# Normalised rows and contexts transposed by VectorE and small transfers instead of TensorE, in a four-layer transformer kernel

## The chip, the cores and the metric

The kernel runs on one core of one Trainium2 chip. The metric is the device time of one execution in microseconds. A core has a matrix engine (TensorE, PE in the profile), a vector engine (VectorE, DVE), an activation engine (ScalarE, ACT), a general engine (GpSimd, POOL), and SyncE (SP), whose queue only issues transfers (DMAs) here. Each engine works through its own instructions in order; semaphores tie the engines to each other.

## The reference

`x` holds 4 batches of 256 tokens with 256 features, `ctx` 4 contexts of 512 tokens with 128 features. Four layers each add a cross-attention and a feed-forward block, both on the normalised rows:

```python
x = x + L0_xattn(layernorm(x), ctx)   # 16 heads of 16, normalised q and k, last 16 context tokens apart
x = x + L0_ffn(layernorm(x))          # 64 "arrows" of rank 16, the 4 longest of each token, and a dense base
x = x + L1_xattn(layernorm(x), ctx)   # 16 heads of 128 on 8 key heads
x = x + L1_ffn(layernorm(x))          # 8 experts, the best 2 of each token, and a shared one
x = x + L2_xattn(layernorm(x), ctx);  x = x + L2_ffn(layernorm(x))   # the better of two experts
x = x + L3_xattn(layernorm(x), ctx);  x = x + L3_ffn(layernorm(x))   # the best 64 tokens of each batch
```

`layernorm` subtracts a row's mean and divides by its standard deviation. All of it is in float32. What matters here: each of these blocks needs the normalised rows with the features on the partitions (a matrix product sums over the partitions), while they are normalised with the tokens on the partitions. Each of the 8 normalised sets of rows must be transposed, batch by batch, and so must each context, once.

## The kernel before

All inputs, the rows `x_sb[b]` (128 partitions x 2 chunks of tokens x 256) and the contexts `c_sb` stay in on-chip memory (SBUF); only weights, and rows for the gathers of the experts, pass through DMA. The order of work on TensorE, ScalarE, VectorE and GpSimd is the order in which `bounded_path` (L837) issues it, by hand. SyncE's order is set by the framework's scheduler, by when a transfer's sources are expected. Transfers of SyncE use eight semaphores in turn, so at most eight are on their way.

**The transposes.** `Norm` (L914) computes a batch's statistics: four small operations of VectorE (L924, L925), one more for the epsilon (L926), and a power on GpSimd (L927). `Norm.tokens` (L929) writes the normalised rows `xn` with two VectorE operations, into a ring of two buffers (pool `lnp`, tag "xn"). `layernorm_T` (L938) transposes them: four matrix products with the identity of 128x128 each (L944) into a PSUM bank, and one ScalarE copy (L947) to `xnT` (128 features x 2 x 256 tokens; a ring of two, tag "xnT"). `context_T` (L906) does the same to a context: four transposes (L910), one copy to `cT`.

**Layer 0, attention.** The loop over batches b and steps i = 0 to 7 issues, in each step, `scores` of half a group of heads (L1371; matrix products L1378, exponentials on ScalarE), the values of the step before (L1388), every second step `quotient` (L1405; VectorE transposes L1411, L1415, multiplication L1419), and then `between(b, i)` (L1589), which prepares batch n = b + 1. For n = 2 and 3, `between` has: at the last two steps of the batch before `Norm` and `tokens`, at i = 0 the transposes of context (`context_T`, then `last_context`, L1176, two GpSimd copies) and of the rows, at i = 1 `project_q` (L1184, products L1189), at i = 2 `project_k` (L1200), at i = 6 `transposed` (L1337; its VectorE part L1353). For n = 1, rows and context are transposed ahead, in part at i = 0. `output0` (L1426) adds a batch's result to `x_sb` (L1438).

**Layer 0, feed-forward.** `Arrows` (L1448; `vectors` with products L1462, `routes`, `turned`, `output` L1512) works on 8 chunks of 128 tokens. Its rows are transposed for batch 0 at (b, i) = (3, 3), batch 1 at (3, 5), batches 2 and 3 in the loop that follows, at n = 1 and 3. Folding of layer 1's weights (L981, `fold`) fills in.

**Layers 1 to 3, attention.** `attention` (L1795) runs over 32 units (b, hp), 4 batches by 8 pairs of heads. A unit takes some 8.4 us and has, on TensorE, `queries` (`seven`, L1893: a 2x2 block product with seven products in place of eight), four scores of 128x512 (L1923) and four products with the context (L1931). For the next batch: `Norm` at hp = 1, `tokens` at hp = 3, `layernorm_T` at hp = 5, `x_sums` (L1855, sums of blocks of `xnT` for `seven`) at hp = 6; `queries` of the next batch follow at hp = 7. VectorE has per unit a transpose of 128x512 (L1952) and sums (L1950, L1956).

**Layer 1, feed-forward.** Its preparation for batches 0 to 2 stands beside layer 1's attention (`beside1`, L2248): `Norm` at hp = 3, `tokens` at hp = 4, `turned1` (L2189) at hp = 5, which stores the rows to `xd` in device memory (L2190) and transposes them (L2195, copy L2196), and at hp = 6 `chosen` (L2198), which computes the gate's products and picks two experts. Batch 3 follows after the attention.

Of the kernel before, what the change touches and what calls it, by code (L numbers as in the profile page):

```python
# [9 lines left out]
F32 = mybir.dt.float32  # L10
# [826 lines left out]
def bounded_path(ctx: ExitStack, tc: tile.TileContext, t, out: bass.AP, over):  # L837
# [8 lines left out]
    first = ctx.enter_context(ExitStack())  # L846
    f0w = first.enter_context(tc.tile_pool(name="f0w", bufs=1, side="right"))
    w0 = first.enter_context(tc.tile_pool(name="w0", bufs=2, side="right"))
    ring = first.enter_context(ExitStack())
    ringo = ctx.enter_context(ExitStack())  # L850
    banks = {
# [99 lines left out]
        xn = Norm(b, name).tokens(keep)  # L951
        return xn, layernorm_T(xn, name)

    def normalised(name):

        after = layernorm(0, f"{name}_0")
        for b in range(B):
            _, xnT = after
            if b + 1 < B:
                after = layernorm(b + 1, f"{name}_{b + 1}")  # L960
            yield b, xnT

    raws = {}

# [68 lines left out]
    with tc.manual_schedule(engines={E.PE, E.Activation, E.DVE, E.Pool}):  # L1033
# [545 lines left out]
        def ahead(b, i):  # L1579

            n = b + 1
            if n < B:
# [3 lines left out]
                elif i == 7 and n > 1:  # L1586
                    transposed(n, 4)

        def between(b, i):  # L1589

            n = b + 1
            if n == 1:
                if i == 0:
                    for k0 in range(0, NK, 2):
                        project_k(n, k0)()
                    scale[n] = Scale(n)
                    scale[n].square(False, NC, NQK)
                    xnTs[n] = layernorm_T(xns[n], f"a0_{n}")
                elif i == 1:
                    project_q(n)()  # L1600
                    scale[n].square(False, 0, NC)
                    project_v(n)
                elif i == 2:
                    scale[n].sum()
                    scale[n].power()
                elif i == 5:
                    transposed(n, 0)
                    transposed(n, 2)
                elif i == 6:
                    transposed(n, 4)  # L1610
            elif n < B:
                if i == 0:
                    context_T(n)
                    last_context(n)
                    xnTs[n] = layernorm_T(xns[n], f"a0_{n}")
                elif i == 1:
                    project_q(n)()
                elif i == 2:
                    for k0 in range(0, NK, 2):
                        project_k(n, k0)()  # L1620
                    scale[n] = Scale(n)
                    scale[n].square(False)
                elif i == 3:
                    project_v(n)
                    scale[n].sum()
                elif i == 4:
                    scale[n].power()
                elif i == 6:
                    transposed(n, 0)
                    transposed(n, 2)  # L1630
            if n + 1 < B:
                if i == (5 if n == 1 else 6):
                    norms[n + 1] = Norm(n + 1, f"a0_{n + 1}")
                elif i == (6 if n == 1 else 7):
                    xns[n + 1] = norms[n + 1].tokens()

            i0 = 4 if b == B - 1 else 6
            if b > 0 and i in (i0, i0 + 1):
                output0(b - 1, (i - i0,))
            if b == 1:  # L1640
                if i == 0:
                    bias_rows()
                elif i == 1:
                    bias_columns()
                elif i == 2:
                    output_bias()
            if b == B - 1:
                if i == 0:

                    mf = w0.tile([B * NK, P], F32, tag="hs", name="mf", bufs=1)  # L1650
                    nc.vector.tensor_copy(mf, m8)
                    xns["mf"] = mf
                elif i == 1:
                    pmk = bank("mm", [P, B * NK], "pmk")
                    nc.tensor.transpose(pmk, xns["mf"], ident[: B * NK, : B * NK])
                    nc.vector.tensor_scalar(
                        mbias.rearrange("p b k -> p (b k)"), pmk, 1.0, -NEG, ALU.subtract, ALU.mult
                    )
                elif i == 2:
                    score_bound()  # L1660
                elif i == 3:

                    nc.vector.tensor_reduce(
                        quad[:, :32], ident.rearrange("p (a q) -> p q a", q=32), AX.X, ALU.add
                    )
                    for j in range(1, 4):
                        nc.vector.tensor_copy(quad[:, 32 * j : 32 * (j + 1)], quad[:, :32])
            if b == B - 1:
                if i in (0, 2, 6):
                    norms["f", i // 2] = Norm(min(i // 2, 2), f"f0_{min(i // 2, 2)}")  # L1670
                if i in (1, 3, 7):
                    xns["f", i // 2] = norms["f", i // 2].tokens()
                if i in (3, 5):
                    k = (i - 3) // 2
                    xnTs["f", k] = layernorm_T(xns["f", k], f"f0_{k}")
                if i == 4:
                    arrows[0] = Arrows(0)
                    arrows[0].vectors()
                if i == 5:
                    arrows[0].routes()  # L1680
# [43 lines left out]
        for n in range(B * NC):  # L1724
            if n + 2 < B * NC:
                arrows[n + 2].routes()
            if n:
                arrows[n].turned()
            if n % NC == 0:
                if n + 3 < B * NC:  # L1730
                    arrows[n + 3] = Arrows(n + 3)
                    arrows[n + 3].vectors()
                for _ in range((0, 0, 1, 1, 2, 2, 1, 1)[n]):
                    next(fold)
                if n == 6:
                    xn1 = norm.tokens()
                if n:
                    arrows[n].output()
            else:
                k = n // NC + 2  # L1740
                if k < B:
                    xnTs["f", k] = layernorm_T(xns["f", k + (k == 2)], f"f0_{k}")
                if n == 7:
                    first_xnT = layernorm_T(xn1, "a1_0")
                    next(fold)
                arrows[n].output()
                for _ in range((0, 0, 1, 1, 2, 2, 1, 0)[n]):
                    next(fold)
                if n + 3 < B * NC:
                    arrows[n + 3] = Arrows(n + 3)  # L1750
                    arrows[n + 3].vectors()
            if n == 5:
                norm = Norm(0, "a1_0")
            if n == 0:
                norm = Norm(3, "f0_3")
            if n == 1:
                xns["f", 3] = norm.tokens()
            if 2 <= n < 2 + B:

                b = n - 2  # L1760
                c2 = w0.tile([P, NK, DC], F32, tag="z0", name=f"c2_{b}")
                for k in range(NK):
                    nc.scalar.activation(
                        c2[:, k], c_sb[:, b, k], AF.Square, accum_out=csq[:, b * NK + k : b * NK + k + 1]
                    )
# [29 lines left out]
    def attention(L, m_sb, n_sb, first_xnT=None, after=None, at_end=None, chunk=None, within=None):  # L1795
# [11 lines left out]


        with tc.tile_pool(name=f"att{L}", bufs=2) as ap:
            xnTs, xns, xxs, norms, qTs, pqs, outs, sums = {}, {}, {}, {}, {}, {}, {}, {}  # L1810
            units = [(b, hp) for b in range(B) for hp in range(H // 2)]
            m_x = ap.tile([P, H // 2, 3, P], F32, tag="m_x", name=f"m_x{L}", bufs=1)
            n_x = ap.tile([P, H // 2, 3, P], F32, tag="n_x", name=f"n_x{L}", bufs=1)
# [220 lines left out]
            for n, (b, hp) in enumerate(units):  # L2034
                if b + 1 < B:
                    if hp == 1:
                        norms[b + 1] = Norm(b + 1, f"a{L}_{b + 1}")
                    elif hp == 3:
                        xns[b + 1] = norms[b + 1].tokens()
                if n == 0:  # L2040
                    first_queries(1)
                    x_sums(0)
                elif n + 1 < len(units):
                    queries(*units[n + 1])
                if b + 1 < B and hp == 5:
                    xnTs[b + 1] = layernorm_T(xns[b + 1], f"a{L}_{b + 1}")
                if b + 1 < B and hp == 6:
                    x_sums(b + 1)
                if b == 0:
# [136 lines left out]
    nc.vector.memset(taken[:, 0, :], 0.0)  # L2186
    xnT1 = {}

    def turned1(b, xn):  # L2189
        nc.sync.dma_start(xd[b * S : (b + 1) * S, :].rearrange("(c p) d -> p c d", p=P), xn)  # L2190
        xnT1[b] = fx.tile([P, ND, S], F32, tag=f"xnT{b}", name=f"xnT_f1_{b}")
        pt = bank("t", [P, ND, S], f"pxn_f1_{b}")
        for c in range(NC):
            for d in range(ND):
                nc.tensor.transpose(pt[:, d, c * P : (c + 1) * P], xn[:, c, d * P : (d + 1) * P], ident)  # L2195
        nc.scalar.copy(xnT1[b], pt)  # L2196
# [51 lines left out]
    def beside1(b, hp):  # L2248
        if b == 0:
            load_waiting(2)  # L2250
        if b > 0:
            if hp == 3:
                ahead1[b] = Norm(b - 1, f"f1_{b - 1}")
            elif hp == 4:
                ahead1[b] = ahead1[b].tokens()
            elif hp == 5:
                turned1(b - 1, ahead1[b])
            elif hp == 6:
                chosen(b - 1)

# [1193 lines left out]
```

## Time and profile before

| | |
|---|---|
| three runs | 1390.88, 1387.66, 1390.79 us (median 1390.79) |
| the profiled execution | 1386.64 us, its span 1384.9 us |
| granted TensorE clock, mean | 0.999 of full speed |
| ScalarE, GpSimd: busy | 580.2 us (42%), 683.9 us (49%) |
| scores of layers 1 to 3 (L1923), 768 products | 345.6 us of TensorE |
| products with the context (L1931), 768 | 345.3 us of TensorE |
| SyncE's queue (q1): packets, megabytes | 46406, 37.69 MB, 8.9% of 16 DMA engines' time |
| all transfers | 47.10 MB, 34 GB/s on average |

The profile is of one execution, and all times within it count from the start of its span. "Busy" is the union of the durations of an engine's instructions, so pipelined matrix products that overlap are counted once. The chain of work follows back from the last instruction to whatever released each step. In a timeline a row gives start, length, engine, line and operation, with tiles out<-in and their shapes; "x4" behind a row means four instructions put together, and the length runs from the first one's start to the last one's end. Rows of SPq are the issues of transfers on SyncE's queue.

### The profile page before, as it was taken

What the parts mean: (1) busy time and instruction counts of PE and PEld (TensorE: products, weight loads), DVE (VectorE), ACT (ScalarE), POOL (GpSimd) and SP (SyncE); (2) the same over time, 40 slices, a digit from 0 to 9 for tenths busy, and PEclk for the clock granted to TensorE, in tenths of its full rate; (3) what the DMA queues carried; (4) which work ended last, traced back from release to release, by engine and by line L of the source; (5) the groups of instructions that cost most, each with busy time, mean ns of one, the idle gap of its engine ahead of it and who ended that gap; (6) DMA issues with size and microseconds to landing.
All of it is one profiled execution on the core that took longest, in us unless ns stands there. A gap on an engine that the chain in (4) does not pass through costs nothing.

```text
span 1384.9 us, 20011 instructions
## 1 busy us (share of the span) xinstructions
PE 1374.5 (99%) x7277; PEld 908.1 (66%) x7277; DVE 887.1 (64%) x2026; ACT 580.2 (42%) x1148; POOL 683.9 (49%) x829
## 2 busy tenths in 40 slices
PE   9999999999999999999999999999999999999998
PEld 7665676566656667887565666666975656666667
DVE  6667863665666547655666756558656758566676
ACT  5766454433343332356434333333364344333331
POOL 4223333566565445232577654556315675445561
PEclk9999999999999999999999999999999999999999
DMA  5000220300000001172110000000332000000001
GB/s 170 2 1 2 76 77 21 78 17 1 9 0 9 1 9 34 47 238 67 39 54 8 16 1 9 0 0 16 120 117 65 8 4 4 0 1 0 1 0 34
DMA packets 50849, 47.10 MB, mean 34 GB/s; under 512 B 8755, under 2 KB 46868, under 8 KB 50742
## 3 DMA queue, kind: packets, MB, share of 16 engines
q1 hardware_dynamic: 46406, 37.69, 8.9%
q0 software_dynamic: 2544, 6.95, 1.8%
q8 instruction: 60, 0.98, 0.3%
q10 hardware_dynamic: 1792, 1.10, 0.3%
q14 instruction: 47, 0.39, 0.1%
HBM read 38.78 MB, written 6.95 MB: 33 GB/s over the span
## 4 chain that ended last, share of the span: by engine, by line
PE 95%; POOL 2%; DVE 1%; DMA 1%; issue 0%; ACT 0%; ACTq 0%; SPq 0%; POOLq 0%; DVEq 0%
PE ps L1923 23%; PE po L1931 23%; PE paq L1893 6%; PE pao L1893 5%; PE pbq L1893 4%; PE pbo L1893 4%; PE ps L1378 3%; PE po L1388 2%; PE pyf L1512 2%; PE paf L1462 2%; PE pgu L2471 2%; PE psh L2292 2%; PE py L2017 2%; PE pn L1008 1%; PE pb L2876 1%; PE pm L992 1%
## 5 line engine op out<-in xcount | busy, mean ns | idle before, releaser
L1942 POOL TENSOR_TENSOR half<-pT 128x1024 f32<-128x1024 f32 x93 | 218.4, 2349 | 287.1 <-ACT pT L1926 214.8
L1923 PE MATMUL ps<-qT,cT 128*128 128x512 f32 x768 | 345.6, 593 | 0.0
L1931 PE MATMUL po<-pT,c_sb 128*128 128x512 f32 x768 | 345.3, 592 | 0.0
L1926 ACT ACTIVATE pT<-ps,mbias 128x512 f32<-128x512 f32 x384 | 263.8, 687 | 155.3 <-PE ps L1923 140.0
L1931 PEld LDWEIGHTS po<-pT,c_sb 128*128 128x128 f32 x768 | 145.8, 190 | 183.2 <-issue 183.2
L1923 PEld LDWEIGHTS ps<-qT,cT 128*128 128x128 f32 x768 | 138.9, 190 | 138.4 <-issue 136.3
L1935 ACT COPY oT<-po 128x512 f32<-128x512 f32 x96 | 56.2, 586 | 265.2 <-PE po L1931 265.2
L1978 POOL TENSOR_TENSOR oT<-oT,wide 128x512 f32<-128x512 f32 x84 | 106.8, 1292 | 0.0
L1903 DVE TENSOR_TENSOR qT<-qT,paq 128x128 f32<-128x128 f32 x90 | 25.5, 283 | 96.0 <-ACT qT L1902 96.0
L1382 ACT ACTIVATE pT<-ps 128x512 f32<-128x512 f32 x128 | 66.0, 602 | 25.8 <-PE ps L1378 25.6
L1950 DVE TENSOR_TENSOR half<-half 128x512 f32<-128x512 f32 x96 | 71.8, 748 | 2.7 <-POOL half L1940 2.5
L1952 DVE STREAM_TRANSPOSE turned<-half 128x512 f32<-128x512 f32 x96 | 68.3, 711 | 6.3
L1903 DVE TENSOR_TENSOR w<-w,pao 128x128 f32<-128x128 f32 x21 | 6.0, 286 | 103.0 <-ACT w L1902 103.0
L1893 PE MATMUL paq<-xnT_a,m_sb 128*128 128x128 f32 x360 | 71.4, 280 | 0.0
L1893 PE MATMUL paq<-xx,m_x 128*128 128x128 f32 x360 | 69.6, 275 | 0.0
L1893 PEld LDWEIGHTS paq<-xnT_a,m_sb 128*128 128x128 f32 x360 | 57.2, 192 | 16.7 <-issue 8.5
L1956 DVE TENSOR_REDUCE sums<-turned 128x16 f32<-128x512 f32 x96 | 65.9, 686 | 3.3
L1893 PE MATMUL pao<-n_x,ox 128*128 128x128 f32 x336 | 65.0, 275 | 0.0
L1902 ACT COPY qT<-paq 128x128 f32<-128x128 f32 x90 | 23.9, 265 | 94.1 <-PE paq L1893 94.1
L1906 DVE TENSOR_TENSOR qT<-qT,pbq 128x384 f32<-128x384 f32 x90 | 49.9, 554 | 9.7 <-DVE qT L1905 0.5
L1893 PEld LDWEIGHTS paq<-xx,m_x 128*128 128x128 f32 x360 | 54.7, 192 | 0.0
L1977 DVE STREAM_TRANSPOSE wide<-rz 128x512 f32<-128x512 f32 x84 | 54.4, 686 | 0.0
(490 smaller groups left out, 2547.3 us busy)
## 6 DMA issues: line engine op xcount, KB each, us to landing
wq<-in_L_wqT SPq DMA_DIRECT2D x11, 512.0 KB, 4.2
wo<-in_L_wo SPq DMA_DIRECT2D x11, 512.0 KB, 5.1
yd<-yr SPq DMA_DIRECT2D x20, 128.0 KB, 3.6
xd<-xn_f SPq DMA_DIRECT2D x8, 256.0 KB, 2.3
w<-in_F_w SPq DMA_DIRECT2D x4, 512.0 KB, 3.3
wk<-in_L_wkT SPq DMA_DIRECT2D x11, 128.0 KB, 4.0
wv<-in_L_wvT SPq DMA_DIRECT2D x11, 128.0 KB, 4.4
yd<-yb SPq DMA_DIRECT2D x9, 128.0 KB, 2.4
```

Source lines behind the costliest of these rows:

```text
L1382: nc.scalar.activation(pT[kp][:, j], ps[j], AF.Exp)
L1893: nc.tensor.matmul(p[:, at, :], lhsT=lhsT, rhs=rhs, start=(k == 0 and at == 0), stop=(k == len(of) - 1 and i == which[-1]),)
L1923: nc.tensor.matmul(ps, lhsT=cT[:, b, k * P : (k + 1) * P], rhs=qT, start=True, stop=True)
L1926: nc.scalar.activation(pT[:, k, :], ps, AF.Exp, bias=mbias[:, b, k : k + 1])
L1931: nc.tensor.matmul(po, lhsT=c_sb[:, b, k, :], rhs=pT[:, k], start=(k == 0), stop=(k == NK - 1))
L1935: done["head"] = nc.scalar.copy(raw, po).ins
L1942: nc.gpsimd.tensor_tensor(half, pT[:, 0:2], pT[:, 2:4], ALU.add)
L1950: nc.vector.tensor_tensor(part, half[:, 0], half[:, 1], ALU.add)
L1952: nc.vector.transpose(turned.rearrange("p f i -> p (f i)"), part)
L1956: nc.vector.tensor_reduce(sums[b, hp // 4][:, hp % 4, :], turned, AX.X, ALU.add)
L1977: nc.vector.transpose(wide, rzs[b, hp // 4][:, hp % 4, :, None].to_broadcast([P, NB, 32]))
L1978: eng.tensor_tensor(outs[b, hp], outs[b, hp], wide.rearrange("p f i -> p (f i)"), ALU.mult)
```

## The change

Twenty groups of four TensorE transposes with their ScalarE copy are replaced by a "turn": VectorE's transpose works on blocks of 32x32, so it turns each block in place and gathers the blocks in a buffer `y`; 16 transfers on SyncE, each of 32 partitions x 128 elements (16 KB, in pieces of 128 bytes), then move the blocks to the partitions where they belong. Changed are

- the contexts of batches 2 and 3 in layer 0 (turned at i = 2 of the batch two before),
- the rows of batches 2 and 3 in layer 0's attention: statistics at i = 4, tokens and turn at i = 5 of the batch before, in place of steps 5 to 7 and transposes at i = 0,
- the rows of all four batches for layer 0's arrows: batch 0 at (2, 6) and (2, 7), batch 1 at (3, 0) and (3, 1), batch 2 at (3, 6) and (3, 7), batch 3 at n = 0 and 1,
- the rows of batches 1 to 3 in the attention of layers 1 to 3, turned at hp = 3 with the tokens,
- the rows of batches 0 to 2 for layer 1's experts, turned at hp = 4 with the tokens.

Rows of each layer's first batch, the contexts and rows of batches 0 and 1 in layer 0, and batch 3 of layer 1's experts stay with TensorE. A context needs one VectorE transpose of 128x512, rows need two of 128x256. In layer 0, `y` and the arrows' rows have a pool of their own (`early`: two `y`, four `xf`); later `y` takes buffers of the ring of `xn`.

```diff
+    early = first.enter_context(tc.tile_pool(name="early", bufs=2, side="right"))
...
+    def squares(shape, name, soon):
+        return early.tile(shape, F32, tag="y", name=name) if soon else lnp.tile(shape, F32, tag="xn", name=name)
+
+    def turned_aside(dst, src, name):
+
+        y = squares([P, 4, 4, 32], f"y_{name}", True)
+        nc.vector.transpose(
+            y.rearrange("p q n s -> p n q s"), src.rearrange("p (n q s) -> p n q s", q=4, s=32)
+        )
+        to = dst.rearrange("p (n i s) -> p i n s", i=4, s=32)
+        for i in range(4):
+            for q in range(4):
+                nc.sync.dma_start(to[32 * q : 32 * q + 32, i], y[32 * i : 32 * i + 32, q])
+
+    def layernorm_aside(xn, name, xnT, soon=False):
+
+        y = squares([P, 4, ND, NC, 32], f"y_{name}", soon)
+        for c in range(NC):
+            nc.vector.transpose(
+                y[:, :, :, c].rearrange("p q d s -> p d q s"), xn[:, c, :].rearrange("p (d q s) -> p d q s", d=ND, s=32)
+            )
+        to = xnT.rearrange("p d (c i s) -> p i d c s", c=NC, s=32)
+        for i in range(4):
+            for q in range(4):
+                nc.sync.dma_start(to[32 * q : 32 * q + 32, i], y[32 * i : 32 * i + 32, q])
+        return xnT
...
+        def rows_of_arrows(k):
+            xnT = early.tile([P, ND, S], F32, tag="xf", name=f"xnT_f0_{k}", bufs=B)
+            xnTs["f", k] = layernorm_aside(norms["f"].tokens(), f"f0_{k}", xnT, True)
...
+            if b == B - 2:
+                if i == 6:
+                    norms["f"] = Norm(0, "f0_0")
+                elif i == 7:
+                    rows_of_arrows(0)
...
             elif n < B:
                 if i == 0:
-                    context_T(n)
                     last_context(n)
-                    xnTs[n] = layernorm_T(xns[n], f"a0_{n}")
...
             if n + 1 < B:
-                if i == (5 if n == 1 else 6):
+                if i == 2:
+                    turned_aside(cT[:, n + 1, :], c_sb[:, n + 1].rearrange("p k c -> p (k c)"), f"c{n + 1}")
+                elif i == 4:
                     norms[n + 1] = Norm(n + 1, f"a0_{n + 1}")
-                elif i == (6 if n == 1 else 7):
-                    xns[n + 1] = norms[n + 1].tokens()
+                elif i == 5:
+                    name = f"a0_{n + 1}"
+                    xnTs[n + 1] = layernorm_aside(norms[n + 1].tokens(), name, rows_tile(name), True)
...
-                if i in (0, 2, 6):
-                    norms["f", i // 2] = Norm(min(i // 2, 2), f"f0_{min(i // 2, 2)}")
-                if i in (1, 3, 7):
-                    xns["f", i // 2] = norms["f", i // 2].tokens()
-                if i in (3, 5):
-                    k = (i - 3) // 2
-                    xnTs["f", k] = layernorm_T(xns["f", k], f"f0_{k}")
+                if i in (0, 6):
+                    norms["f"] = Norm(1 + i // 6, f"f0_{1 + i // 6}")
+                if i in (1, 7):
+                    rows_of_arrows(1 + i // 6)
...
                     elif hp == 3:
-                        xns[b + 1] = norms[b + 1].tokens()
+                        name = f"a{L}_{b + 1}"
+                        xnTs[b + 1] = layernorm_aside(norms[b + 1].tokens(), name, rows_tile(name))
...
-                if b + 1 < B and hp == 5:
-                    xnTs[b + 1] = layernorm_T(xns[b + 1], f"a{L}_{b + 1}")
...
             elif hp == 4:
-                ahead1[b] = ahead1[b].tokens()
-            elif hp == 5:
-                turned1(b - 1, ahead1[b])
+                turned1(b - 1, ahead1[b].tokens(), True)
```

## The prediction

> **What bounds the kernel.** I read the page's busy times first, then its chain, then TensorE's timeline around each group of transposes.
>
> ```profile
> PE 1374.5 (99%) x7277; PEld 908.1 (66%) x7277; DVE 887.1 (64%) x2026; ACT 580.2 (42%) x1148; POOL 683.9 (49%) x829
> PE 95%; POOL 2%; DVE 1%; DMA 1%; issue 0%; ACT 0%; ACTq 0%; SPq 0%; POOLq 0%; DVEq 0%
> ```
>
> TensorE is busy all the time and is 95% of the chain; its longest wait, in the list of waits, is 1.5 us. So what TensorE no longer does is saved, and each microsecond it newly waits is lost. Matmuls overlap, so the price of a transpose is not its duration (273 ns) but the distance between starts:
>
> ```profile
> 347.28 0.39 PE L1893 MATMUL pbq<-xx,m_sb 128*128 128x128 f32 x2
> 347.51 0.60 PE L944 MATMUL pxn_a<-ident,xn_a 128*128 128x128 f32 x4
> 347.94 1.02 PE L1923 MATMUL ps<-qT,cT 128*128 128x512 f32 x2
> ```
>
> From 347.51 to 347.94: four transposes cost 0.44 (unrounded), 0.11 apiece.
>
> **What goes.** The order of the instructions confirms that 20 groups of four transposes leave TensorE and nothing joins it. By the distance from each group's start to the next work:
> - layer 0, batch 2: 48.76 to 49.78, 1.02 for context and rows; batch 3: 80.69 to 82.28, 1.59 (with a wait of 0.34 for VectorE);
> - layer 0's experts: 0.58 (at 119.77) + 0.53 (130.41) + 2 x 0.44 = 1.99;
> - layers 1 to 3, attention: 9 x 0.44 = 3.96; layer 1's experts, batches 0 to 2: 3 x 0.44 = 1.32.
>
> Sum 1.02 + 1.59 + 1.99 + 3.96 + 1.32 = **9.9 us**. The 20 copies on ScalarE that go (some 0.6 each) hide beside TensorE and bring nothing. The Trainium skill, "TensorE: Matmul & The Clock Gate", Part 4, gives some 275 ns for a transpose in one kernel's context. That is near this trace's duration; used as a price it would give an estimate of 80 x 0.275 = 22 us, but the starts 0.11 apart decide.
>
> **What comes.** A turn is one or two VectorE transposes and 16 transfers of 16 KB on SyncE's queue, and the reader needs the last of them.
> - VectorE: 128x512 takes 0.71 (L1952); two halves, not in the trace, 0.36 to 0.5 each, I take 0.4: 0.8 a turn, 16 us in all. VectorE idles a third of the time and TensorE reads its results a unit later.
> - Issue: the nearest row is eight small loads in a row.
>
> ```profile
> 11.64 4.22 SPq L1080 DMA_DIRECT2D wo<-in_L_wo  x8
> ```
>
> The first seven start 0.47 apart (x8 ends at 15.86 only because the last waits for a semaphore). Unhindered issues elsewhere lie 0.41 to 0.6 apart. Bounds 0.41 and 0.6 (the four-dimensional pattern may cost more); I take 0.47, the nearest shape.
> - Landing: bounds 1.6 (gw, 256 pieces of 32 bytes, nothing else in flight) and 2.9 (median of those eight, beside big loads); I take 1.7, as nothing else is in flight in layer 0 then.
>
> So a turn lasts 15 x 0.47 + 1.7 = **8.75 us** after VectorE is done. The Trainium skill, "DMA: Bandwidth & Descriptors", Rules for kernel authors, speaks against this: coalesce small transfers, since below 64 KB one pays mostly overhead. Here the overhead is harmless wherever the turn has time, so I go by deadlines.
>
> **Deadlines that hold.** Layers 1 to 3: rows are ordered in unit 3, and x_sums first reads them in unit 6, three units of 8.43 us later: 25.3 against 0.8 + 0.8 + 8.75 = 10.4 (tokens, transposes, transfers); cover left 15. Layer 1's experts: xd is issued at 347.49, the gate products start at 363.3: 15.8 against 10, cover 6. The "xn" ring of two now alternates rows and turned rows; a slot comes back after two units, 17 us, again more than 10. On SyncE the turn of batch 1 stands between weight loads of the same layer; those slip by less than a unit and are first read hundreds of microseconds (layer 1) or many units later. Layer 0's experts, batch 3: VectorE ends the rows at 169.99, turned 170.8, landed 179.6; first read 182.27 - 0.44 = 181.8: cover 2.2. It stands on SyncE before the raw weights of 181.6, so delays none. Batch 0: rows now follow the quotient that ends at 111.2 and Norm's four statistics before it find VectorE idle; turned 112.8, landed 121.6; first read 123.40 - 0.58 = 122.8: cover 1.2. Batches 1 and 2 have over 8 us. Layer 0's contexts are turned at (0,2) and (1,2), five steps early.
>
> **Deadlines that don't hold: layer 0's rows 2 and 3.** They are read by project_q at L1189:
>
> ```profile
> 48.76 0.66 PE L910 MATMUL pcT<-ident,c_sb 128*128 128x128 f32 x4
> 49.25 0.60 PE L944 MATMUL pxn_a<-ident,xn_a 128*128 128x128 f32 x4
> 49.78 1.37 PE L1378 MATMUL ps<-qT,kT 32*128 32x256 f32 x16
> ...
> 52.51 0.70 PE L1189 MATMUL pq<-wq,xnT_a 128*128 128x256 f32 x2
> ```
>
> Without the first two, TensorE wants these rows at 52.51 - 1.02 = 51.5. VectorE before:
>
> ```profile
> 42.24 0.69 DVE L1419 TENSOR_TENSOR o<-po,z 128x512 f32<-128x512 f32 x1
> 42.85 0.80 DVE L1353 TENSOR_SCALAR qT<-pT,cols 128x512 f32<-128x512 f32 x1
> 43.57 0.42 DVE L924 BATCH_NORM_STATS2 st_a<-x_sb 128x6 f32<-128x256 f32 x1
> ```
>
> After, the statistics stand ahead of that quotient (they push it by 0.3), and behind qT come tokens (0.73, from the row at 45.91) and transposes (0.8): 43.95 + 0.73 + 0.8 = 45.5. Landed 45.5 + 8.75 = 54.2, 2.8 after 51.5: **TensorE waits 2.8**. Behind that matmul its whole queue waits, the next scores and so ScalarE; nothing gives it back. Batch 3: quotient ends at 73.84, tokens 74.5, turned 75.3, landed 84.1; wanted at 84.79 - 1.59 = 83.2: **0.9**. Sum of stalls 3.7.
>
> By the bounds: issue 0.41 and landing 1.6 give 45.5 + 6.15 + 1.6 - 51.5 = 1.8 and none: 1.8. Issue 0.6: 10.7 a turn, 4.7 + 2.9, and layer 0's experts' batch 0 misses by 0.7: 8.3. Landing 2.9 alone: 4.0 + 2.1 = 6.1.
>
> **A cold clock.** A TensorE gap of 3 us is not in this trace after its start (the longest is 1.2), but the start shows what a restart costs:
>
> ```profile
> 5.53 1.06 PE L910 MATMUL pcT<-ident,c_sb 128*128 128x128 f32 x4
> 7.23 0.60 PE L944 MATMUL pxn_a<-ident,xn_a 128*128 128x128 f32 x4
> ```
>
> The same four transposes take 0.85 from start to start at 5.53 and 0.44 at 7.23; the first matmul was at 1.5, the change at 6.8. A restart thus loses 0 to half of 5.3 = 2.6 us. At a stall of 2.8 I take 0, and keep 2.6 for the range. The Trainium skill, "TensorE: Matmul & The Clock Gate", Why this matters for your kernels, warns of idle gaps over some 3 us, after which the array runs at half clock. With its window of 3.4 us an estimate of the loss would be 1.7 us, and a 2.8 us stall would be just inside.
>
> **Sum.** -9.9 + 2.8 + 0.9 = **-6.2 us**. The profiled execution took 1386.64 (span 1384.9 and 1.7 around it), so it would become 1380.4. The median of the three runs, 1390.79, lies 4.2 above that execution; I subtract from the median: **1384.6**.
>
> **Rivals.** A measurement of this kernel tells 0.3%, 4.2 us, from no change.
> - Turns in time (0.15): issue 0.41, landing 1.6 or better: -9.9 + 1.8 = -8.1, at best -9.9: 1382.7 to 1380.9. For it: nothing else loads SyncE in layer 0. Against: TensorE reaches project_q only 6 us after VectorE finishes.
> - Stalls eat most of it (0.30): issue 0.6, -9.9 + 8.3 = -1.6, 1389.2; with one cold restart +1.0, 1391.8. Landing 2.9 alone, -3.8, 1387.0. For it: issues of wider patterns are the slower ones.
> - Slower (0.13): SyncE's interval itself. Every turn with a short deadline pays 15 times it. Gain and stalls balance at 0.63 (0.57 with one restart). At 0.8 (the slowest issues, beside big loads, took that) a turn is 13.7: stalls 7.7 + 5.9 + 3.7 + 2.7 = 20, so +10 without restarts, 1401. Against: those had loads in flight.
> - The forecast, -4.2 to -8, holds 0.42.
>
> **Range and chances.** 1380.9 (all of the gain) to 1392 (slow issue with a restart): outside lies most of the slower case and a little below. Faster by over 0.3%: 0.42 + 0.15 = 0.57. Within 0.3%: 0.30. Slower: 0.13.
>
> **What would show it.** Right: TensorE's busy time falls by some 10 and the 80 transposes are gone; its largest new waits stand before L1189's successor twice, near 51 (about 3) and near 83 (about 1), released by transfers; 16 issues of a turn 0.47 apart; the nine attention turns land units ahead of x_sums. Wrong: intervals over 0.6, or transposes at twice 0.11 after the first stall (cold); VectorE waiting for transfers in the rings; a wait of TensorE at 122 or 181; any new wait in layers 1 to 3.

## The result, and the profile after

The changed kernel took **1400.68 us** (median of six runs, 1398.91 to 1404.43), the kernel before 1388.92 us beside it (six runs, 1386.23 to 1390.88). The ratio is **1.0097**, with a 95% interval of 1.0084 to 1.0109: slower by 12 us (medians) to 13 us (ratio), where 1384.6 was predicted. The profiled execution has a span of 1399.1 us, 14.2 more than that of before, whose profiled execution (1386.64) is 2.3 us faster than its median.

From `project_q` on, lines of the changed kernel are 22 to 26 higher: `project_q` multiplies at L1211, the scores of layer 0 are L1400, `Arrows.vectors` L1484, `queries` L1919, the scores of layers 1 to 3 L1949.

What was to be gained is there. At the place of the first timeline of the prediction (layer 1, batch 1), the scores now start 0.22 us after the last two products of `queries`, with no transposes between:

```profile
362.92 0.39 PE L1919 MATMUL pbq<-xx,m_sb 128*128 128x128 f32 x2
363.14 1.02 PE L1949 MATMUL ps<-qT,cT 128*128 128x512 f32 x2
```

Set side by side, product by product, TensorE's two timelines differ by -0.44 us at each of the 12 turns of layers 1 to 3 and of layer 1's experts, by -1.02 and -1.58 at layer 0's batches 2 and 3, and by -0.59 and three times -0.44 at layer 0's arrows: 9.8 us less in all. TensorE's waits in the changed kernel (microseconds in total, times, longest) tell where more than that went:

```profile
PE pq L1211 <- DMA xnT_a<-y_a: 9.8, 2, 6.0
PE paf L1484 <- DMA xnT_f<-y_f: 3.1, 2, 1.9
PE pgu L2497 <- ACT xgT L2474: 1.6, 2, 0.8
...
PE pT L1368 <- DVE qT L1375: 1.4, 2, 0.7
...
PE ps L1400 <- DVE y_sb L1460: 0.7, 1, 0.7
```

The first two are new and wait for transfers. Here is the longest, on SyncE's queue (first row) and on TensorE:

```profile
45.84 10.24 SPq L979 DMA_DIRECT2D xnT_a<-y_a  x16
```

```profile
51.02 0.61 PE L1419 MATMUL po<-pT,vals_d 128*32 128x256 f32 x8
57.61 3.75 PE L1211 MATMUL pq<-wq,xnT_a 128*128 128x256 f32 x8 [5.98 <-DMA xnT_a<-y_a]
61.29 0.75 PE L1345 MATMUL pbrow<-ident,bval 1*128 1x1 f32 x3
```

The turn starts when predicted (45.84; predicted 45.5). Its 16 issues take 10.24 us; they start 0.64 apart. The last landing is at 57.30, 11.5 us after the first issue, where 8.75 was reckoned. The eight products behind then take 3.75 us. In the row of before the same products started 0.22 apart; now they start 0.43 apart. The table of stretches shows why, in the column after POOL, the granted clock:

```profile
57.60:62.00 4.40, 4.39 (x15) 3.19 (x19) 0.60 (x1) 0.00 (x0) 0.00 (x0) 0.51 0.01 4
62.00:66.00 4.00, 4.00 (x43) 2.84 (x40) 1.20 (x3) 2.06 (x4) 0.00 (x0) 1.00 0.00 0
```

After the wait of 6 us TensorE ran at half clock for some 4 us. Batch 3's turn ends in the same way, with the second wait:

```profile
95.30 3.08 PE L1211 MATMUL pq<-wq,xnT_a 128*128 128x256 f32 x8 [3.86 <-DMA xnT_a<-y_a]
```

The ledger of the 14.2 us, from the two timelines laid side by side:

| place | us |
|---|---|
| transposes gone | -9.8 |
| wait at `project_q`, batch 2 and batch 3 | +6.05, +3.9 |
| half clock behind these two waits | +1.95, +1.6 |
| waits at the arrows' vectors, batch 0 and batch 3 | +1.4, +2.0 |
| TensorE later because VectorE is later, layer 0 | +0.8, +0.8, +1.3 |
| layer 1's experts, gathered rows (waits for ScalarE) | +1.1 |
| from TensorE's last product to the end | +2.1 |
| steps under 0.25 us | +1.0 |

### The profile page after: what moved, and what is told of

It reads as the page before. It is cut to its first block, busy times and chain, and to the rows that moved or that the text cites. A ratio compares the mean times of both kernels' runs of the same rounds, so it can differ in the third digit from the quotient of the medians.

```text
span 1399.1 us, 20322 instructions
## 1 busy us (share of the span) xinstructions
PE 1371.1 (98%) x7197; PEld 902.4 (64%) x7197; DVE 902.2 (64%) x2064; ACT 569.0 (41%) x1128; POOL 683.5 (49%) x829
## 3 DMA queue, kind: packets, MB, share of 16 engines
q1 hardware_dynamic: 92486, 42.95, 11.5%
## 4 chain that ended last, share of the span: by engine, by line
PE 52%; POOL 2%; DVE 1%; issue 0%; ACT 0%; ACTq 0%; DVEq 0%; POOLq 0%
PE ps L1949 15%; PE po L1957 15%; PE paq L1919 4%; PE pao L1919 3%; PE pbq L1919 3%; PE pbo L1919 3%; PE pb L2902 1%; PE py L2043 1%; PE pm L1014 1%; PE pn L1030 1%; PE pyb L2928 1%; PE pgu L2497 1%; PE ph L3281 1%; PE pq L1901 0%; PE po L3296 0%; POOL oT L2004 0%
## 5 line engine op out<-in xcount | busy, mean ns | idle before, releaser
L1949 PE MATMUL ps<-qT,cT 128*128 128x512 f32 x768 | 345.6, 593 | 0.0
L1949 PEld LDWEIGHTS ps<-qT,cT 128*128 128x128 f32 x768 | 138.9, 190 | 138.4 <-issue 136.3
L1919 PE MATMUL paq<-xnT_a,m_sb 128*128 128x128 f32 x360 | 71.3, 280 | 0.0
L1919 PE MATMUL paq<-xx,m_x 128*128 128x128 f32 x360 | 69.6, 275 | 0.0
L1919 PEld LDWEIGHTS paq<-xnT_a,m_sb 128*128 128x128 f32 x360 | 57.5, 192 | 18.2 <-issue 9.2
L1919 PE MATMUL pao<-n_x,ox 128*128 128x128 f32 x336 | 65.0, 275 | 0.0
L1919 PEld LDWEIGHTS paq<-xx,m_x 128*128 128x128 f32 x360 | 54.7, 192 | 0.0
```

Source lines behind the costliest of these rows:

```text
L1919: nc.tensor.matmul(p[:, at, :], lhsT=lhsT, rhs=rhs, start=(k == 0 and at == 0), stop=(k == len(of) - 1 and i == which[-1]),)
L1949: nc.tensor.matmul(ps, lhsT=cT[:, b, k * P : (k + 1) * P], rhs=qT, start=True, stop=True)
```

## The experiments

Three theories. **A, the issue in a row:** 16 issues of 0.64 us make a turn too long for readers that come soon, above all `project_q`. **B, VectorE:** its added work in layer 0 delays its old work, and that delays TensorE. **C, the transfer:** pieces of 128 bytes move slowly, whoever issues them.

**e1: layer 0's rows of batches 2 and 3 back on TensorE.** All else stays turned.

```diff
                     last_context(n)
+                    xnTs[n] = layernorm_T(xns[n], f"a0_{n}")
...
-                elif i == 4:
-                    norms[n + 1] = Norm(n + 1, f"a0_{n + 1}")
-                elif i == 5:
-                    name = f"a0_{n + 1}"
-                    xnTs[n + 1] = layernorm_aside(norms[n + 1].tokens(), name, rows_tile(name), True)
+                if i == (5 if n == 1 else 6):
+                    norms[n + 1] = Norm(n + 1, f"a0_{n + 1}")
+                elif i == (6 if n == 1 else 7):
+                    xns[n + 1] = norms[n + 1].tokens()
```

> The changed kernel, but layer 0's rows of batches 2 and 3 go back to TensorE at the steps they had before; the contexts and all other rows stay turned. Theory A (16 issues of 0.64 us in a row, and a reader only some 5 us behind, make project_q wait): the waits of 6.0 and 3.8 us at project_q and the slow matrix products behind them (about 1.8 and 1.4 us) go, two groups of transposes come back at 0.44 to 0.8 each, so 11 to 12 us less than the changed kernel: ratio to before 0.999 to 1.002. Theory B (VectorE's added work delays its other work in layer 0): only the delay of some 0.8 us before step (1, 7) goes, ratio 1.009. Theory C (the slow part is the transfer of 128-byte pieces itself, anywhere): the other turns would cost too, ratio above 1.004.

Measured: 1389.39 us, ratio 1.0008 (0.9996 to 1.0019). Two turns of twenty thus account for about nine tenths of the loss against before, as A has it; B alone would have kept 1.009. What is left is seen in its profile: at the arrows' vectors TensorE still loses 1.35 us (batch 0), and for batch 3 a wait of 2.8 with 1.6 of half clock behind it.

**e2: all of layer 0 as before**, only the twelve turns of layers 1 to 3 left (`between` and the loop over n are those of before).

> The changed kernel with all of layer 0 as before; only the 9 turns in the attention of layers 1 to 3 and the 3 for layer 1's experts stay. Theory A: 12 times 0.44 = 5.3 us less than before, no new wait of TensorE for a transfer, ratio 0.996. The profile of the changed kernel also shows 1.1 us more at the experts' gathered rows of layer 1 (waits for ScalarE's copy) and 2.1 us more between TensorE's last product and the end. If these come from the turns they are seen here again, ratio 0.9985; if they come from where the code happens to lie, they may be absent or stand elsewhere. Theory C: TensorE waits at x_sums or at the gate's products, ratio 1.0 or above.

Measured: 1383.02 us, ratio 0.9957 (0.9943 to 0.9970). TensorE waits for no transfer, and each of the twelve places gives 0.44 us, so C falls for these: the same 16 transfers cost nothing where there is time. In the profiled execution layer 1's experts lost 3.1 us against before, in other places than in the changed kernel (once 1.5 us behind ScalarE's `yr`), and the end was 1.8 us longer than before's; both are taken up below. That execution (1386.29) was the slowest of five; the other four took 1382.6 to 1383.1.

**e3: everything turned, but earlier in layer 0.** Rows of batches 2 and 3 at i = 2; the context of batch 2 with TensorE again.

```diff
-                if i == 2:
-                    turned_aside(cT[:, n + 1, :], c_sb[:, n + 1].rearrange("p k c -> p (k c)"), f"c{n + 1}")
-                elif i == 4:
+                if i == n - 1:
                     norms[n + 1] = Norm(n + 1, f"a0_{n + 1}")
-                elif i == 5:
+                elif i == 2:
                     name = f"a0_{n + 1}"
                     xnTs[n + 1] = layernorm_aside(norms[n + 1].tokens(), name, rows_tile(name), True)
+                elif i == 4 and n == 2:
+                    turned_aside(cT[:, n + 1, :], c_sb[:, n + 1].rearrange("p k c -> p (k c)"), f"c{n + 1}")
...
-                if i == 6:
+                if i == 2:
                     norms["f"] = Norm(0, "f0_0")
-                elif i == 7:
+                elif i == 3:
                     rows_of_arrows(0)
...
+        norms["f"] = Norm(3, "f0_3")
         for n in range(B * NC):
...
             if n == 0:
-                norms["f"] = Norm(3, "f0_3")
-            if n == 1:
                 rows_of_arrows(3)
```

> All turns of the changed kernel but one (the context of batch 2 is back on TensorE), those of layer 0 ordered earlier: rows of batch 2 at (0, 2), rows of batch 3 at (1, 2), context of batch 3 at (1, 4), arrows' rows of batch 0 at (2, 3), of batch 3 at the end of n = 0. Theory A: nothing is late any more, the waits at project_q and at the arrows' vectors go (6.0 + 3.8 + 3.1 us and the slow products behind two of them), so 9.9 - 0.6 = 9.3 us less than before, ratio 0.9933; with the 3.2 us of the end and of layer 1's experts still there 0.9956. Theory B: VectorE's added work costs wherever it stands, some 3 us in layer 0, ratio 0.9955 to 0.998 with waits of TensorE for VectorE at other places. A wait for a transfer at project_q would show that the turn is longer than 12 us.

Measured: **1380.72 us**, ratio 0.9948 (0.9934 to 0.9962): better than both kernels. In its profile TensorE goes from the values to `project_q` without a wait:

```profile
51.37 0.61 PE L1419 MATMUL po<-pT,vals_d 128*32 128x256 f32 x8
51.91 1.99 PE L1211 MATMUL pq<-wq,xnT_a 128*128 128x256 f32 x8
```

TensorE waits for no transfer anywhere. Up to its last product it is 7.8 us ahead of before, of 9.3 that were to be had; 1.6 us of VectorE's delays in layer 0 show where B is right: at a product that waits for the bias rows (0.57), in batch 2's step 6 (0.6) and at the arrows (0.4).

**e4 and e8: the transfers and the restart by themselves.** Two kernels that leave out the whole computation.

> The kernel leaves out the whole computation; it measures transfers between SBUF tiles by themselves, then TensorE's restart after gaps. On SyncE: 16 of the change's shape (32 partitions, 4 pieces of 128 bytes each, dturn), 16 of 32 partitions x 512 bytes in one piece (dwhole), 16 of 32 x 128 bytes (dsmall), 4 of 128 partitions x 512 bytes (dtall), 4 of 128 partitions x 4 pieces of 128 bytes (dcut), then 16 of the change's shape on ScalarE's queue (dact), on both queues by turns (dboth) and on GpSimd's (dpool). Theory A, the issue sets the pace: dturn 0.64 apart; dboth half as long as dturn; landing 1.8 us after the issue throughout. If the issue goes by the number of pieces, dwhole and dsmall lie 0.4 to 0.5 apart and dcut above 1 us; if by the instruction, all lie within 0.1 of 0.64. Theory C, the pieces' own transfer sets it: landing grows along dturn and dboth ends no earlier. Restart: bursts of 70 products of 128x256 (0.22 us apart at full clock, 0.43 at half) with growing gaps; the changed kernel lost some 1.4 us after a gap of 4.2 us and 1.9 after one of 6.4, nothing after 1.9. The same is expected here: nothing below some 2.5 us, then up to about 2 us.

SyncE's and GpSimd's queues in the first probe (start, length of all issues together; a tall transfer has 128 partitions and 64 KB, a small one 4 KB):

```profile
3.75 10.49 SPq L69 DMA_DIRECT2D dturn<-sturn  x16
14.36 10.27 SPq L76 DMA_DIRECT2D dwhole<-swhole  x16
24.73 10.61 SPq L83 DMA_DIRECT2D dsmall<-ssmall  x16
35.44 2.47 SPq L89 DMA_DIRECT2D dtall<-stall  x4
38.00 2.69 SPq L97 DMA_DIRECT2D dcut<-scut  x4
```

```profile
6.37 8.78 POOL L69 DMA_DIRECT2D dpool<-spool  x16 [5.93 <-DVE spool L58]
```

ScalarE's queue:

```profile
5.43 10.48 ACTq L69 DMA_DIRECT2D dact<-sact  x16
```

The issue on SyncE takes 0.64 us, whether it moves 4 KB, 16 KB or 64 KB, in pieces of 128 or 512 bytes (0.68 for the tall one in pieces of 128). It is paid by the instruction. On GpSimd's queue the interval is 0.54, on ScalarE's 0.66. SyncE's half of `dboth` ran long after ScalarE's, so that group compares nothing; but the first groups of the three queues ran at the same time, from 6.4 to 14.2 us, and SyncE kept its 0.64. Landing rose from 1.8 to 2.3 us along `dturn` meanwhile; in the second probe, where SyncE issues alone, it stays at 1.8 with the same interval. So the moving of the bytes did not set the pace, and C falls.

> The kernel leaves out the whole computation. The first probe had every issue between SBUF tiles at 0.64 us, whatever its pieces and size, while the loads that the prediction took its 0.47 from come from device memory. 16 transfers each on SyncE's queue: device memory to SBUF (dfromdram), SBUF to device memory (out), SBUF to SBUF across lanes (down) and on the same lanes (dlanes), all 32 rows x 512 bytes, and SBUF to SBUF with 16 rows x 1 KB (dsixteen). If the place of the ends sets the interval: dfromdram 0.47, out between, down and dlanes 0.64. If the count of rows does: dsixteen below 0.64 and dfromdram at 0.64. Then TensorE's restart again, gaps of 3.0 to 5.8 us, several of each, after bursts of different lengths: the first probe lost 0 at 3.0, 1.6 at 3.5, 0 at 3.9, 1.7 at 4.9 and 6.7. If the loss goes by the gap alone, equal gaps lose equally; if by where the gap lies against some clock of its own, equal gaps between 3.4 and 6 lose 0 or 1.6.

```profile
3.95 10.08 SPq L76 DMA_DIRECT2D down<-sown  x16
14.07 5.22 SPq L113 DMA_DIRECT2D dfromdram<-in_x  x11
19.41 8.42 SPq L118 DMA_DIRECT2D out<-stodram  x16
27.93 10.02 SPq L123 DMA_DIRECT2D dlanes<-slanes  x16
```

It is the place of the ends: 0.63 apart between SBUF tiles (also on the same lanes, and with 16 rows in place of 32), 0.46 from device memory, and 0.46 to it (one issue of 1.6 lies in the row). The row that the prediction took, weights from device memory, could not show the interval of this transfer.

The restart: after bursts of TensorE the same gap costs different amounts. In the second probe three gaps of 3.46 us (start to start) lost 0, 1.7 and 0 us; four of 3.92 lost 1.7, 2.7, 0 and 2.9; those of 4.4 to 5.8 lost 1.7 to 2.9; 3.0 lost nothing. The clock granted in the first 3.15 us behind the three gaps of 3.46 (the column after POOL):

```profile
75.45:78.60 3.15, 3.15 (x15) 2.79 (x16) 0.00 (x0) 0.00 (x0) 1.00 0.00 0
111.61:114.76 3.15, 3.15 (x8) 2.52 (x9) 0.00 (x0) 0.00 (x0) 0.50 0.00 0
150.75:153.90 3.15, 3.15 (x15) 2.79 (x16) 0.00 (x0) 0.00 (x0) 1.00 0.02 5
```

So the loss does not go by the gap's length alone. The Trainium skill, "TensorE: Matmul & The Clock Gate", Part 1, What's actually happening, says that the clock gate's window of some 3.4 us runs freely and is not reset when the kernel starts. The traces agree. In each of the twelve profiles all changes of the granted clock, from the first to the last, lie on one grid with steps of 3.41 us, and within the work TensorE goes back to half clock for one step or two (3.41 or 6.83 us). Laid over this grid, the 43 waits of TensorE of over 1.4 us behind the first change separate cleanly: the 28 that cover 0.63 or more of one step are followed by half clock, the 15 that cover 0.58 or less of any step are not. By their length they do not: the shortest with half clock is 2.4 us (in e6), the longest without it 3.55.

**e5: two queues.** Of the 16 transfers of layer 0's rows of batches 2 and 3, eight go through GpSimd's queue.

```diff
-    def layernorm_aside(xn, name, xnT, soon=False):
+    def layernorm_aside(xn, name, xnT, soon=False, queues=(nc.sync,)):
...
-                nc.sync.dma_start(to[32 * q : 32 * q + 32, i], y[32 * i : 32 * i + 32, q])
+                queues[q % len(queues)].dma_start(to[32 * q : 32 * q + 32, i], y[32 * i : 32 * i + 32, q])
...
-                    xnTs[n + 1] = layernorm_aside(norms[n + 1].tokens(), name, rows_tile(name), True)
+                    xnTs[n + 1] = layernorm_aside(
+                        norms[n + 1].tokens(), name, rows_tile(name), True, (nc.sync, nc.gpsimd)
+                    )
```

> The changed kernel with one thing other: of the 16 transfers of layer 0's rows of batches 2 and 3, eight go through SyncE's queue and eight through GpSimd's, in the same place of the program. By the measurement of the transfers alone, an issue takes 0.64 us on SyncE's queue and 0.54 on GpSimd's. Theory A (the 16 issues in a row): a turn of these rows takes 7 x 0.64 + 1.9 = 6.4 us in place of 11.5, so project_q waits about 1 us for batch 2 in place of 6.0, and not at all for batch 3, with no slow products behind them: some 12 us less than the changed kernel, ratio to before 0.998 to 1.001. Theory C (the pieces' transfer or the landing sets it): no change, ratio 1.009. What may eat some of it: GpSimd stands still for 8 x 0.54 = 4.3 us, with its sums of the heads behind.

Measured: 1389.43 us, ratio 1.0007 (0.9997 to 1.0017), as A reckoned. SyncE's queue, GpSimd and TensorE:

```profile
45.72 5.10 SPq L979 DMA_DIRECT2D xnT_a<-y_a  x8
```

```profile
46.30 4.67 POOL L979 DMA_DIRECT2D xnT_a<-y_a  x8 [1.56 <-DVE kT L1386]
```

```profile
53.04 1.32 PE L1211 MATMUL pq<-wq,xnT_a 128*128 128x256 f32 x5 [1.53 <-DMA xnT_a<-y_a]
```

The same bytes, pieces and places, only issued side by side: the wait falls from 5.98 to 1.53, batch 3's is gone, and so is the half clock behind them. The arrows' turns are still on one queue: there TensorE waits 4.5 us in this profile (3.1 in the changed kernel), with some 1.8 us of half clock behind the longer wait, of 2.9. The Trainium skill, "DMA: Bandwidth & Descriptors", Rules for kernel authors, holds that spreading transfers over queues brings no bandwidth and only saves the issue time; here the issue time is the whole matter.

**e6: the attention's turns two units later** (`hp == 3` becomes `hp == 5`, tokens included), to see whether the cover of layers 1 to 3 is real.

> The changed kernel with tokens and turn of the rows in the attention of layers 1 to 3 two units (16.9 us) later, at hp = 5. In the changed kernel the rows of batch 1 of layer 1 land at 278.5 and are first read by VectorE at 292.6: a cover of 14.1. Two units later they land 2.8 us after VectorE wants them. Theory A, with covers counted to the first reader on TensorE: VectorE waits some 1 to 5 us at x_sums nine times, but TensorE needs the sums only in the next unit, so the time stays that of the changed kernel within 0.1% (ratio 1.009 to 1.011). If VectorE's wait reaches TensorE through its other work (sums of halves, queries), 9 times 1 to 5 us: ratio 1.015 to 1.04.

Measured: 1447.03 us, ratio 1.0425 (1.0406 to 1.0443), 46 us more than the changed kernel. The expectation that TensorE would not notice was wrong; the measured ratio lies just above the other one, 1.015 to 1.04. VectorE's waits:

```profile
DVE xx L1850 <- DMA xnT_a<-y_a: 37.5, 9, 6.4
...
DVE y_a L973 <- DMA xnT_f<-y_f: 19.4, 2, 9.8
```

VectorE waits 4.2 us on average at each of the nine sums. In six of the nine batches (two of layer 1, three of layer 2, one of layer 3) VectorE's delay reaches TensorE, which takes its results one unit later; by the two timelines each of them loses 5 to 10 us, half clock included. The second row is a wait for a buffer: in layer 1 the experts' `y` still sits in the ring of two when the attention's `y` wants it. So the cover of 14 us that the changed kernel shows there (rows of batch 1 landed at 278.53, first read at 292.64) is what makes the turns free, and it ends abruptly.

**e7: the changed kernel once more**, for its profile.

> The changed kernel once more, for its profile alone: the 6.0 and 3.8 us at project_q must be there again within 0.3 us. Open are 1.1 us at the gathers of layer 1's experts and 2.1 us more after TensorE's last product. If they stand there again they belong to this code; if they are other ones, they are of one execution and no part of the change.

The waits at `project_q` are 10.0 us in total, the longest 6.0, and those at the arrows 3.4: they belong to the code. At layer 1's gathers this execution is 1.7 us faster than the other of the same code, so that term belongs to the execution. The end is again long, 7.0 us from the last product, against 7.3 and 5.2 before.

**e9: the way through device memory.** Eight transfers of 64 KB in place of 16 of 16 KB, everything else where the change put it.

```diff
+        z = [aside.tile([P, P], F32, tag=f"z{i}", name=f"z{i}_{name}") for i in range(4)]
+        for i in range(4):
+            nc.sync.dma_start(
+                z[i].rearrange("(q r) m -> r q m", r=32), y[32 * i : 32 * i + 32].rearrange("r (q m) -> r q m", q=4)
+            )
+        for i in range(4):
+            nc.sync.dma_start(to[:, i], z[i].rearrange("p (n s) -> p n s", s=32))
```

(`aside` is a pool of device memory, with four tiles of 128 x 128 for a turn.)

> The changed kernel, but a turn goes through device memory: four transfers of 32 partitions write the blocks there (pieces of 512 bytes), four of 128 partitions read them back into place (pieces of 128 bytes); everything stands where it stood. The second probe had issues with one end in device memory 0.46 us apart, and between SBUF tiles 0.63. Theory A: a turn takes 7 x 0.46 + 1.6 to 2.1 = some 5.2 us from first issue to last landing (the first write has landed when the first read is issued), in place of 11.5, so project_q waits 0 to 0.5 us in place of 6.0 and 3.8, the arrows' vectors nothing in place of 3.1, and no slow products follow: some 15 us less than the changed kernel, ratio to before 0.995 to 0.9985. VectorE's delays in layer 0 (2.9 us) stay. If the pieces (twice as many bytes now) set the pace, the turn is as long or longer: ratio 1.009 or more.

Measured: 1384.61 us, ratio 0.9973 (0.9963 to 0.9982). A turn takes 6.6 us (first issue 45.68, landed 52.24) and not 5.2, since the reads with 128 partitions and four pieces each are issued 0.62 to 0.67 apart and the last lands 2.7 us after its issue, where 1.6 to 2.1 was taken. `project_q` waits 0.9 us for batch 2 and nothing for batch 3:

```profile
45.68 1.76 SPq L965 DMA_DIRECT2D z_a<-y_a  x4
47.61 2.55 SPq L969 DMA_DIRECT2D xnT_a<-z_a  x4
```

```profile
52.49 1.97 PE L1218 MATMUL pq<-wq,xnT_a 128*128 128x256 f32 x8 [0.90 <-DMA xnT_a<-z_a]
```

In place of the other queue or the other time, a shorter turn: a third way to the same end. VectorE's delays (0.8, 0.8 and 1.3 us) are unchanged, as B's part should be.

**e10: both**, e3's order with e9's transfers; batch 2's context is turned too, and layer 0's statistics and turns stand behind the bias work of their step.

> The earlier turns of layer 0 together with the way through device memory; the context of batch 2 is turned as well, at (0, 4), and the statistics and turns of layer 0 stand behind the bias work of their step. Theory A: everything is in time, all of the 9.9 us are there but for up to 1 us of VectorE's delays: ratio 0.9925 to 0.994, that is 0 to 3 us below the kernel with earlier turns alone, and not clearly apart from it. Waits of TensorE for transfers: none.

Measured: 1382.64 us, ratio 0.9960 (0.9948 to 0.9972), not apart from e3, and above the 0.9925 to 0.994 expected. TensorE waits for no transfer and is 8.1 us ahead of before at its last product, but the end took 7.1 us in place of 5.2: that is what lies between 8.1 and the 6.4 us of the medians.

## Why the prediction was wrong

- **What goes: right.** 9.9 reckoned from distances of starts, 9.8 measured. The transposes' durations (0.27) would have misled.
- **Issue, 0.47: the step that failed.** "Unhindered issues elsewhere lie 0.41 to 0.6 apart" had bounds from transfers with one end in device memory (before has no others on this queue). Between SBUF tiles it is 0.64, and eleven of the twenty turns hold one issue of 1 us or more (before had four such too, of 1.1 to 2.4 us; 0.8 was not its slowest), so that layer 0's eight turns average 0.68. With 0.68 the prediction's own sum gives a turn of 15 x 0.68 + 1.7 = 11.9 and stalls of 5.9 (measured 6.05), 4.0 (3.9), 1.9 (1.4) and 0.9 (2.0): 12.7, not 3.7. The net would have been +2.8, not -6.2. The way from there to the profiles' +14.2 is half clock (3.55), VectorE (2.9), the end (2.1), layer 1's experts (1.1), small steps (1.0) and 0.7 more of stalls.
- **Landing, 1.7: right** (1.8).
- **Deadlines: right in which, but the small covers fell.** Layer 0's rows 2 and 3 are the late ones, at the places named; layers 1 to 3 and layer 1's experts wait for nothing. The covers of 1.2 and 2.2 at the arrows were smaller than the error of the turn and became losses of 1.4 and 2.0.
- **Cold clock, taken as 0: wrong**, 3.55 us in two places. The bound of 2.6 each held here (the second probe lost up to 2.9). Both waits had grown past 3 us, but 0 was not safe at 2.8 either: in e1 a wait of 2.6 us was followed by half clock, in e6 waits of 2.4 and 2.5.
- **VectorE, costed at nothing: wrong by 2.9 us.** "TensorE reads its results a unit later" is true of layers 1 to 3. In layer 0 little lies between VectorE's work and its reader: in the changed kernel, rows of batch 3 and their transposes stand ahead of `qT`, which TensorE's next transposes wait for:

```profile
80.88 1.14 DVE L933 TENSOR_SCALAR xn_a<-x_sb,mv_a,rstd_a 128x256 f32<-128x256 f32 x2
81.94 0.76 DVE L973 STREAM_TRANSPOSE y_a<-xn_a 128x256 f32<-128x256 f32 x2
82.62 0.76 DVE L1375 TENSOR_SCALAR qT<-pT,cols 128x512 f32<-128x512 f32 x1
```

- **Rivals.** The rival "slower" named the mechanism, the place and the point (0.63, or 0.57 with a restart; its own sum gives 0.58) from which it decides; 0.64 to 0.68 is just beyond. It had 0.13, on the ground that the slow issues seen had loads in flight. Near a break-even of 0.6 with an unknown between 0.41 and 0.8 it deserved far more.
- **What stays open.** The end after TensorE's last product took 5.2 us before, 5.3 in e1, and 6.4 to 7.3 in the profiles of all the others, the changed kernel's two among them. Most of the difference is the jump over the path that is not taken: SyncE went on 0.5 us after its branch in before and 2.9 in the changed kernel. What decides it was not found; it is up to 2 us of the 13. Layer 1's experts, with their gathers, ran between 0.3 us shorter and 3.1 us longer than before in eight profiles. In four of these (e1, e2, e5, e9) 1.7 us of it is one step of half clock just behind 32 small products (128x40, L2404 of before) that take 3.8 us and start at most 0.3 apart. Laid over the clock's grid, these products fill 0.84 or more of one step in the four, and 0.74 or less in before, the changed kernel's two, e3 and e10, where the clock stays full. The rest differs from execution to execution, and its cause is open.

## What to carry to other kernels

Before transfers replace work on the bottleneck engine, measure the interval of issues for that very kind of transfer, with both ends where they will lie: it times the number of transfers in a row, and the landing of the last, is the length of the step. Then set it against the reader's deadline at each place; twenty edits of one kind were worth some 0.5 us each here (9.8 in all), and two of them cost 13.5 us together, since a late one stops TensorE's whole queue and, if the wait is long, halves its clock for a while. If a deadline is short, order the step earlier, split the issues over queues, or use fewer transfers; all three worked.

## What the runs showed of the hardware

- An issue on SyncE's queue: 0.63 to 0.64 us between SBUF tiles, for 4 KB as for 64 KB (0.68 for 512 pieces); 0.46 with one end in device memory (32 rows of 512 bytes), 0.62 to 0.67 there for reads of 512 pieces. On GpSimd's queue 0.54.
- TensorE's clock after a gap (start to start, both probes): nothing lost at 3.0 us, between 0 and 2.9 us at gaps of 3.5 and 3.9, and 1.7 to 2.9 at 4.4 to 6.7. What decided it in these profiles is how much of one step of a grid of 3.41 us the wait covers: half clock at 0.63 and more, none at 0.58 and less. In the changed kernel the second wait, of 3.9 us, was followed by four products at full clock before the half clock set in.
- The two normalising operations of VectorE took 0.73 us in a row of before where GpSimd was idle and 3.16 us in e3 while GpSimd worked (59.57 to 62.42). The Trainium skill, "GPSIMD Engine Reference", Key points, has the two engines share their SBUF interfaces, which fits.
